# A graph network in fp32 on one core: the last block's products with the adjacency matrix on four row tiles

## The chip, the core and the metric

The kernel runs on one core of a Trainium2 chip. Its engines are named as the profile names them: PE (matrix products; PEld is its weight load), DVE (vector), ACT (scalar), POOL (GpSimd) and SP (here only a queue for DMAs). The metric is device time in microseconds (us).

## What is computed

Four layers in a row on 2708 nodes with 512 features. `adj` is a symmetric matrix of zeros and ones, 2708 x 2708, with about 0.6% ones. Cut to what matters:

```python
deg = jnp.maximum((adj != 0).sum(-1), 1.0)
# layer 0: degree-normalised sum over neighbours, times W, relu
x = layernorm(x + relu(((dinv * (adj + I) * dinv) @ x + x) @ W0 + b0))   # dinv: degree per row
# layer 1: the same with both sides scaled by deg ** -0.5
x = layernorm(x + ((dis * adj * dis) @ x) @ W1.T + b1)
# layer 2: two attention layers, softmax(scores) * adj, then @ Wh
x = layernorm(x + gat(gat(x)))
# layer 3: adj @ (H W) per head plus b, heads side by side
x = layernorm(x + adj @ (x @ W3) + b3)
```

Layers 0, 1 and 3 each hold one product of `adj` with the whole of `x`. The change is about these three products.

## The kernel before

**Tiling.** The 2708 nodes make 22 blocks of 128 rows (`NB`, `P`); block 21 has only 20 real rows (2708 - 21 x 128) and is padded with zeros. The output columns of a product with `adj` come in six chunks (`CH`): four of 512 columns, one of 384, one of 276. The 512 features are four groups (`DC`) of 128, numbered d. The 22 blocks are loaded in six groups (`GROUPS`): four of 4 blocks, two of 3. Block 21 is the last of group 5.

**The product.** `multiply` (L813) builds, for a chunk k, the four banks `acc[k][d]` (128 features x the chunk's columns), each summed over all 22 blocks. The weights are 128 columns of a block of x, the moving data are the block's rows of adj.T, cast to fp32r (tile `m`). To keep fp32 precision x is split by `halve` (L705) into two fp32r halves: `hi` (ACT, tiles named xh) and `lo = x*s - hi` (DVE, tiles named xl). Each block thus costs 4 x 2 = 8 products a chunk. In group 5 the products run d by d: for every d the blocks 19, 20, 21, each hi then lo. In chunk 0 the other groups run block by block.

**Loads.** `load` (L716) brings adj.T. In layer 0 it comes as fp32, one DMA of SP's queue per block, into a tile `at`; the pool of these tiles (`wides`) has 11 buffers, so a load waits until an older tile is free. In layers 1 and 3 it comes as bytes, one DMA per group, from `masks`, which layer 0 has written to memory.

**Preparing.** `prepare` (L749) casts `at` to `m` on ACT and, in chunk 0, calls `halve`. In layer 0 `examine` (L780) also makes bf16 copies (`some`, ACT), checks on DVE that all values are 0 or 1 (`odd`), makes the bytes for `masks` (POOL) and adds the blocks up into `part` (DVE), from which `degrees` (L836) gets the node degrees: `both` on DVE, a product with ones on PE (`deg`), then `dg` on DVE, then xt * dg on POOL, which `evict` (L869) adds to `acc` on DVE, giving `ht`. In layer 1 `prepare` also reduces the bytes to `feeds` (DVE), which says which 32-wide quarter of a block a node feeds.

**Order.** The order of issue on each engine is written out by hand: every instruction goes through `OrderedEngine` (L62), whose call on L70 keeps the order, which is why nearly all rows of the profile carry L70. `step` (L993) works through (layer, chunk, group): it loads two groups ahead and prepares one group ahead (`before_products`, L962), multiplies, and in between finishes the chunk before (`ends`, L1027: `project` gives the products mm with W, `combine` and `finish` the bias, the residual and the layer norm). In layer 3, chunks 0 to 2 begin while the attention layers end: groups 0 to 3 are multiplied early and saved to `begun`, groups 4 and 5 are added after.

**Tiles of the array.** `few` (L645) already uses a part of the array: where a block has at most 32 output rows, four products run on four column tiles (each a different quarter of the output partitions) and `total` adds the four parts. The lists of neighbours in `weigh` do the same with quarters of 32 rows.

Of the kernel before, what the change touches and what calls it, by code (L numbers as in the profile page):

```python
# [8 lines left out]
FP = mybir.dt.float32  # L9
# [10 lines left out]
P = 128  # L20
N = 2708
D = 512
NB = 22
NP = NB * P
DC = D // P
# [11 lines left out]
QUARTERS, QW = 4, P // 4  # L37
# [476 lines left out]
class Fast:  # L514
# [190 lines left out]
    def halve(self, ly, j):  # L705

        nc = self.nc
        hi = self.page(f"xh{ly.number}_{j}", FR)
        lo = self.page(f"xl{ly.number}_{j}", FR)
        s = self.k.dis[:, j : j + 1] if ly.number == 1 else 1.0  # L710
        x = ly.rows[j]
        nc.scalar.activation(hi, x, AF.Copy, scale=s)
        nc.vector.scalar_tensor_tensor(lo, x, s, hi.bitcast(FP), ALU.mult, ALU.subtract)
        ly.hi[j], ly.lo[j], ly.rows[j] = hi, lo, None

    def load(self, ly, k, g):  # L716

        c0, cw = CH[k]
        if (k, g) in ly.loaded:
            return  # L720
        ly.loaded.add((k, g))
        js = range(*GROUPS[g])
        if ly.number == 0:
            tiles = []
            for j in js:
                at = self.wide(f"at{ly.number}_{k}_{j}")
                self.nc.sync.dma_start(at[:, :cw], self.k.adj_t[bass.ts(j, P), c0 : c0 + cw])
                tiles.append(at)
        else:
            at = self.page(f"at{ly.number}_{k}_{g}", U8, (P, DC, BANK))  # L730
            self.nc.sync.dma_start(
                at[:, : len(js), :cw], self.k.masks[k][:, js[0] : js[-1] + 1, :]
            )
            tiles = [at[:, q, :] for q in range(len(js))]
            ly.done["bytes", k, g] = at
        ly.done["at", k, g] = tiles
        if k == 0 and ly.number == 0:
            for j in range(*GROUPS[g]):
                self.load_rows(ly, j)
        if k == 0 and ly.number == 3 and g < 4:  # L740
            for j in range(*GROUPS[g]):
                self.load_rows(ly, j)
        if ly.number == 0 and g == 2:
            xt = [self.page(f"xt{k}_{c}") for c in range(DC)]
            for c in range(DC):
                self.nc.gpsimd.dma_start(xt[c][:, :cw], self.k.x_t[:, c, c0 : c0 + cw])
            ly.done["xt", k] = xt

    def prepare(self, ly, k, g):  # L749


        nc, (c0, cw) = self.nc, CH[k]
        ats = ly.done.pop(("at", k, g), None)
        if ats is None:
            return
        ms = []
        for j, at in zip(range(*GROUPS[g]), ats):
            if k == 0:
                self.halve(ly, j)
            m = self.page(f"m{ly.number}_{k}_{j}", FR)  # L760
            nc.scalar.copy(m[:, :cw], at[:, :cw])
            ms.append(m)
        ly.done["m", k, g] = ms
        if ly.number == 0:
            self.examine(ly, k, g, ats)
        if ly.number == 1:
            at, (j0, j1) = ly.done.pop(("bytes", k, g)), GROUPS[g]
            feeds = self.k.feeds.rearrange("p i q j -> p j (i q)")
            i0, full = c0 // QW, cw // QW
            for q0, q1, n in ((0, full, QW), (full, -(-cw // QW), cw % QW)):  # L770
                if q0 < q1:
                    v = at[:, : j1 - j0, q0 * QW : q0 * QW + (q1 - q0) * n]
                    nc.vector.tensor_reduce(
                        feeds[:, j0:j1, i0 + q0 : i0 + q1],
                        v.rearrange("p j (q i) -> p j q i", i=n),
                        AX.X,
                        ALU.max,
                    )

    def examine(self, ly, k, g, ats):  # L780
        nc, cw = self.nc, CH[k][1]
        b0 = GROUPS[g][0]
        if g == 0:
            ly.part[k] = self.page(f"part{k}", BF, (P, 2, BANK))
        odd = self.page(f"odd{k}_{g}", BF)
        at_b = self.page(f"bytes{k}_{g}", U8, (P, DC, BANK))
        for q in range(0, len(ats), 2):
            some = self.page(f"some{k}_{g}_{q}", BF, (P, 2, BANK))
            m = min(2, len(ats) - q)
            for h in range(m):  # L790
                at = ats[q + h][:, :cw]
                n = k * NB + b0 + q + h
                nc.scalar.copy(some[:, h, :cw], at)
                nc.vector.scalar_tensor_tensor(
                    odd[:, :cw],
                    at,
                    1.0,
                    at,
                    ALU.is_equal,
                    ALU.not_equal,  # L800
                    accum_out=self.k.bad[:, n : n + 1],
                )
            nc.gpsimd.tensor_copy(at_b[:, q : q + m, :cw], some[:, :m, :cw])
            p = ly.part[k][:, :m, :cw]
            if b0 + q == 0:
                nc.vector.tensor_copy(p, some[:, :m, :cw])
            else:
                nc.vector.tensor_add(p, p, some[:, :m, :cw])
        nc.gpsimd.dma_start(
            self.k.masks[k][:, b0 : b0 + len(ats), :], at_b[:, : len(ats), :cw]  # L810
        )

    def multiply(self, ly, k, g, only=None):  # L813
        nc, cw = self.nc, CH[k][1]
        blocks = only or range(*GROUPS[g])
        two = ly.number == 3 and k < TWO
        starts, stops = ((0, 16), (15, NB - 1)) if two else ((0,), (NB - 1,))
        if blocks[0] in starts:

            half = 0 if two and blocks[0] == 0 else k  # L820
            ly.acc[k] = [self.bank(half, f"acc{ly.number}_{k}_{d}") for d in range(DC)]
        ms = ly.done["m", k, g]
        todo = [(d, j) for d in range(DC) for j in blocks]
        if k == 0 and g + 1 < len(GROUPS):
            todo.sort(key=lambda a: a[1])
        for d, j in todo:
            for x, first in ((ly.hi, True), (ly.lo, False)):
                nc.tensor.matmul(
                    ly.acc[k][d][:, :cw],
                    x[j][:, bass.ts(d, P)],  # L830
                    ms[j - GROUPS[g][0]][:, :cw],
                    start=(j in starts and first),
                    stop=(j in stops and not first),
                )
# [955 lines left out]
```

## Time and profile before

| what | value |
|---|---|
| median of 3 runs | 2413.58 us (2408.57 to 2414.01) |
| the profiled execution's own time | 2413.0 us |
| its span in the profile | 2411.3 us |
| granted PE clock, mean | 0.982 |
| layer 0, by the products' places in the timeline | 19 to 312 us |
| layer 1 | 312 to 617 us |
| attention, with early parts of layer 3 between | 618 to 2184 us |
| the rest of layer 3 | 2190 to 2396 us |
| products acc<-m,xh and acc<-m,xl | 1584 each, 588.7 and 574.5 us busy |

In the page, a group of instructions has its name as output<-inputs, its shape (for a product: rows*columns of the weights, then partitions x elements of the moving data), its count, its busy time, the mean of one, and the engine's idle time ahead of it with what ended it. The profile counts each fp32 product as two passes; an fp32r product is one. In a timeline the first two columns are the start and the length in us, and merged rows carry a count; "[0.31 <-ACT m]" is idle time ahead of the instruction and what ended it. "SPq" is SP's DMA queue.

### The profile page before, as it was taken

To read this page: it belongs to the slowest core of one execution; us is meant where nothing else is said; L and a number is where in the kernel's file an instruction comes from. 1 tells how busy PE (TensorE), PEld (TensorE's weight loads), DVE (VectorE), ACT (ScalarE), POOL (GpSimd) and SP (SyncE) were. 2 spreads that over 40 slices of the span, in tenths; PEclk is the share of its full clock that TensorE was granted. 3 is DMA by queue.
4 is the path that set the end of the run, shared out by engine and by line. 5 is a ranking of instruction groups with operands and counts; after the bars stand their busy time and mean duration, and the time that the engine had idled before them with its cause. 6 is when DMAs were issued, how large, how long until landed. Compare 5 with 4: busy or idle time off the path is not lost.

```text
span 2411.3 us, 26147 instructions
## 1 busy us (share of the span) xinstructions
PE 2305.6 (96%) x8518; PEld 1322.7 (55%) x8518; DVE 1475.1 (61%) x2842; ACT 653.8 (27%) x1300; POOL 770.3 (32%) x895
## 2 busy tenths in 40 slices
PE   8999999999999998999998999999999998899997
PEld 6677777777545443443554444444443454566685
DVE  7989984756535688757665511247868785623513
ACT  6444352321110122222222210123223233421121
POOL 6545541111000001634556450001643657451000
PEclk9999999999999999999999999999999998899999
DMA  9755552223454114868889895314967889872311
GB/s 349 253 182 165 175 174 77 77 75 110 150 189 181 47 53 126 297 224 284 269 292 353 269 387 207 130 40 154 325 215 270 307 273 345 247 251 93 115 54 41
DMA packets 311126, 471.74 MB, mean 196 GB/s; under 512 B 59874, under 2 KB 189418, under 8 KB 310980
## 3 DMA queue, kind: packets, MB, share of 16 engines
q1 hardware_dynamic: 249684, 236.61, 29.9%
q0 software_dynamic: 61296, 233.37, 28.0%
q8 instruction: 69, 1.13, 0.2%
q14 instruction: 77, 0.63, 0.1%
HBM read 316.01 MB, written 153.85 MB: 195 GB/s over the span
## 4 chain that ended last, share of the span: by engine, by line
PE 80%; DVE 10%; issue 3%; DMA 3%; ACT 1%; POOL 1%; SPq 1%; another core or an unknown queue 1%; DVEq 0%; ACTq 0%; POOLq 0%
PE acc L70 30%; PE sp L70 26%; PE mm L70 9%; PE wst L70 6%; PE z L70 6%; DVE s L70 2%; DVE sum L70 1%; SPq L70 1%; DMA pairs<-s 1%; DVE top L70 1%; DMA at<-in_adj_t 1%; DVE at_row L70 1%; DMA xt<-t 1%; DVE st L70 1%
## 5 line engine op out<-in xcount | busy, mean ns | idle before, releaser
L70 POOL DMA_INDIRECT g<-pairs,givers x510 | 516.3, 1012 | 955.5 <-issue 624.5
L70 PE MATMUL sp<-xs,wst_sb 128*128 128x512 f32 (+3 forms) x2112 | 805.2, 547 | 0.0
L70 PE MATMUL acc<-m,xh 128*128 128x512 f32 (+2 forms) x1584 | 588.7, 378 | 27.5 <-ACT begun L70 14.0
L70 PEld LDWEIGHTS sp<-xs,wst_sb 128*128 128x128 f32 (+1 forms) x2112 | 382.1, 187 | 403.4 <-issue 338.3
L70 PE MATMUL acc<-m,xl 128*128 128x512 f32 (+2 forms) x1584 | 574.5, 368 | 4.1 <-DVE xl L70 3.3
L70 PEld LDWEIGHTS acc<-m,xh 128*128 128x128 f32 x1584 | 301.7, 190 | 89.2 <-ACT begun L70 16.1
L70 PEld LDWEIGHTS acc<-m,xl 128*128 128x128 f32 x1584 | 302.2, 191 | 52.4 <-issue 6.2
L70 PE MATMUL acc<-g 128*32 128x512 f32 (+1 forms) x1020 | 265.2, 610 | 10.0 <-DMA g<-pairs,givers 7.9
L70 ACT COPY s<-sp 128x512 f32<-128x512 f32 (+2 forms) x252 | 132.8, 529 | 469.2 <-PE sp L70 311.2
L70 DVE TENSOR_TENSOR top<-top,s 128x512 f32<-128x512 f32 (+5 forms) x240 | 149.5, 623 | 161.2 <-ACT s L70 112.4
L70 PE MATMUL mm<-w,ht 128*128 128x512 f32 (+1 forms) x528 | 226.1, 600 | 7.7 <-DVE ht L70 7.7
L70 ACT ACTIVATE s<-s 128x512 f32<-128x512 f32 (+3 forms) x264 | 150.4, 580 | 294.4 <-DVE s L70 204.7
L70 ACT CAST m<-at 128x512 fp32r<-128x512 uint8 (+5 forms) x396 | 199.1, 567 | 68.0 <-DMA at<-mask 42.3
L70 DVE TENSOR_TENSOR sum<-sum,s 128x512 f32<-128x512 f32 (+4 forms) x252 | 156.8, 622 | 39.4 <-issue 20.9
L70 DVE TENSOR_TENSOR s<-s,a 128x512 f32<-128x512 f32 (+3 forms) x264 | 165.9, 628 | 9.1
L70 DVE TENSOR_TENSOR s<-s,shift 128x512 f32<-128x512 f32 (+3 forms) x264 | 162.8, 620 | 10.3 <-ACT shift L70 10.3
L70 PEld LDWEIGHTS mm<-w,ht 128*128 128x128 f32 (+1 forms) x528 | 96.9, 188 | 126.6 <-issue 112.3
L70 PEld LDWEIGHTS acc<-g 128*32 128x32 f32 (+1 forms) x1020 | 77.1, 136 | 147.4 <-issue 125.0
L70 PE MATMUL wst<-xt,mixed 128*128 128x512 f32 (+2 forms) x384 | 150.5, 545 | 1.7 <-issue 1.7
L70 PE MATMUL z<-w,xt 128*128 128x512 f32 (+1 forms) x352 | 150.2, 595 | 0.0
L70 DVE COPY z_sb<-z 128x512 f32<-128x512 f32 (+1 forms) x44 | 30.3, 690 | 175.8 <-PE z L70 130.8
L70 POOL DMA_DIRECT2D x<-o x44 | 25.9, 595 | 349.8 <-DVE o L70 346.1
(159 smaller groups left out, 1662.0 us busy)
## 6 DMA issues: line engine op xcount, KB each, us to landing
pairs<-s SPq DMA_DIRECT2D x378, 128.0 KB
pairs<-z_sb SPq DMA_DIRECT2D x84, 512.0 KB
at<-in_adj_t SPq DMA_DIRECT2D x88, 256.0 KB
xres<-x POOLq DMA_DIRECT2D x44, 256.0 KB
x<-o POOLq DMA_DIRECT2D x43, 256.0 KB
x<-x POOLq DMA_DIRECT2D x35, 256.0 KB
at<-mask SPq DMA_DIRECT2D x32, 256.0 KB
xt<-t SPq DMA_DIRECT2D x32, 256.0 KB
```

The source lines that it names most:

```text
L70: ins = call(*args, **kw)
```

## The change

The products of block 21 are done on four row tiles of the array. Its weights use only the first 32 partitions (20 of them real rows), so the four feature groups d are laid on the four quarters of the partitions:

- `fold` copies columns d x 128 to (d + 1) x 128 of block 21's first 32 rows to partitions d x 32 to (d + 1) x 32 of a new page (four ACT copies a layer); in layer 1 the scale `dis` is laid out likewise by four DVE copies. `halve` then works on 128 columns of this page for both halves, not on 512.
- In layer 0 the first 32 rows of block 21's adj.T are loaded four times, once on each quarter (four DMAs of 32 rows in place of one of 128). The bytes in `masks` then hold the four copies, and layers 1 and 3 load them as they did.
- `multiply` issues the eight products of block 21 ahead of the rest of group 5: four hi products, d = 0 to 3, each with 32 partitions of weights and of adj.T and with its own bank, then four lo products. Blocks 19 and 20 follow d by d. The group's last product is now that of block 20.
- `examine` adds only 32 partitions of block 21 to `part`, and `prepare` reduces block 21 to `feeds` by instructions of its own, so that the copies don't count.

```diff
@@ halve
+        if j == NB - 1:
+            x, s = self.fold(ly, x, s)
+            hi, lo = hi[:, :P], lo[:, :P]
         nc.scalar.activation(hi, x, AF.Copy, scale=s)
         nc.vector.scalar_tensor_tensor(lo, x, s, hi.bitcast(FP), ALU.mult, ALU.subtract)
         ly.hi[j], ly.lo[j], ly.rows[j] = hi, lo, None
+
+    def fold(self, ly, x, s):
+        nc = self.nc
+        f = self.page(f"fold{ly.number}")[:, :P]
+        for d in range(DC):
+            nc.scalar.copy(f[d * QW : (d + 1) * QW], x[:QW, bass.ts(d, P)])
+        if ly.number == 1:
+            t = self.small.tile([P, 1], FP, tag="dis_f", name="dis_f")
+            for d in range(DC):
+                nc.vector.tensor_copy(t[d * QW : (d + 1) * QW], s[:QW])
+            s = t
+        return f, s
@@ load
-                self.nc.sync.dma_start(at[:, :cw], self.k.adj_t[bass.ts(j, P), c0 : c0 + cw])
                 tiles.append(at)
+                if j < NB - 1:
+                    self.nc.sync.dma_start(
+                        at[:, :cw], self.k.adj_t[bass.ts(j, P), c0 : c0 + cw]
+                    )
+                    continue
+                few = self.k.adj_t[j * P : j * P + QW, c0 : c0 + cw]
+                for d in range(DC):
+                    self.nc.sync.dma_start(at[d * QW : (d + 1) * QW, :cw], few)
@@ prepare
+            sets = [(j0, j1, P)] if j1 < NB else [(j0, j1 - 1, P), (j1 - 1, j1, QW)]
             for q0, q1, n in ((0, full, QW), (full, -(-cw // QW), cw % QW)):
-                if q0 < q1:
-                    v = at[:, : j1 - j0, q0 * QW : q0 * QW + (q1 - q0) * n]
+                for a, b, rows in sets if q0 < q1 else ():
+                    v = at[:rows, a - j0 : b - j0, q0 * QW : q0 * QW + (q1 - q0) * n]
                     nc.vector.tensor_reduce(
-                        feeds[:, j0:j1, i0 + q0 : i0 + q1],
+                        feeds[:rows, a:b, i0 + q0 : i0 + q1],
@@ examine
-            p = ly.part[k][:, :m, :cw]
+            n = QW if b0 + q == NB - 1 else P
+            p, t = ly.part[k][:n, :m, :cw], some[:n, :m, :cw]
@@ multiply
-        starts, stops = ((0, 16), (15, NB - 1)) if two else ((0,), (NB - 1,))
+        starts, stops = ((0, 16), (15, NB - 2)) if two else ((0,), (NB - 2,))
         ms = ly.done["m", k, g]
+        if blocks[-1] == NB - 1:
+            blocks = blocks[:-1]
+            for x in (ly.hi, ly.lo):
+                for d in range(DC):
+                    few = slice(d * QW, (d + 1) * QW)
+                    nc.tensor.matmul(
+                        ly.acc[k][d][:, :cw],
+                        x[NB - 1][few],
+                        ms[-1][few, :cw],
+                        start=False,
+                        stop=False,
+                    )
```

More of the change, by code (lines that the diff above doesn't have):

```diff
@@ L803, in examine @@
             nc.gpsimd.tensor_copy(at_b[:, q : q + m, :cw], some[:, :m, :cw])
-            p = ly.part[k][:, :m, :cw]
+            n = QW if b0 + q == NB - 1 else P
+            p, t = ly.part[k][:n, :m, :cw], some[:n, :m, :cw]
             if b0 + q == 0:
-                nc.vector.tensor_copy(p, some[:, :m, :cw])
+                nc.vector.tensor_copy(p, t)
             else:
-                nc.vector.tensor_add(p, p, some[:, :m, :cw])
+                nc.vector.tensor_add(p, p, t)
         nc.gpsimd.dma_start(
```

## The prediction

> **What bounds the kernel now.** First the page's shares of busy time, to see which engine could be the bound:
> ```profile
> span 2411.3 us, 26147 instructions
> PE 2305.6 (96%) x8518; PEld 1322.7 (55%) x8518; DVE 1475.1 (61%) x2842; ACT 653.8 (27%) x1300; POOL 770.3 (32%) x895
> ```
> PE is busy in 96% of the span, so work taken off PE counts unless another engine ends that stage. Next the groups by shape give the size of what is edited; only the rows for the high halves are shown, those for the low halves have the same counts:
> ```profile
> L70 PE MATMUL acc<-m,xh 128*128 128x512 f32 x1056 | 430.1, 407 | 27.5 <-ACT begun L70 14.0 <-ACT m L70 8.6 <-DVE dg L70 4.9
> L70 PE MATMUL acc<-m,xh 128*128 128x384 f32 x264 | 89.9, 341 | 0.0
> L70 PE MATMUL acc<-m,xh 128*128 128x276 f32 x264 | 68.7, 296 | 0.0
> ```
> The mean of one (407 ns) holds latency that overlaps. The pitch is read from the chain that ended last, where whole runs of these products stand:
> ```profile
> 90.81 32.69 PE acc L70 x144
> ...
> 252.88 24.99 PE acc L70 x144
> ...
> 2369.89 18.48 PE acc L70 x144
> ```
> 32.69/144 = 0.227 us at 512 columns, 24.99/144 = 0.1735 at 384, 18.48/144 = 0.128 at 276. These runs are on the chain from end to end: there PE waits for nobody.
>
> **What is removed.** In each of 3 layers x 6 chunks, block 21 has 4 (d) x 2 (halves) = 8 products. At the pitches they take 8 x 0.227 = 1.82 us (12 chunks of 512), 1.39 (3 of 384), 1.03 (3 of 276): 29.0 us in all. They become two rounds of four products, each on 32 rows, each of the four into its own PSUM bank.
>
> **What a round costs.** No row of this trace has four row tiles. The nearest is the kernel's own set of four column tiles (`few`, 20 rows): same array, split the other way, fp32 in two passes. The timelines around one, of weight loads and of matmuls:
> ```profile
> 330.86 0.19 PEld L70 LDWEIGHTS mm<-w,ht 128*128 128x128 f32 x1 [0.24 <-issue]
> 331.81 0.14 PEld L70 LDWEIGHTS mm<-w,ht 128*20 128x20 f32 x8 [0.76 <-issue]
> 332.80 0.19 PEld L70 LDWEIGHTS acc<-m,xh 128*128 128x128 f32 x1 [0.85 <-issue]
> ```
> ```profile
> 331.29 1.58 PE L70 MATMUL mm<-w,ht 128*128 128x512 f32 x9
> 332.80 0.50 PE L70 MATMUL acc<-m,xh 128*128 128x512 f32 x1
> 333.13 0.40 PE L70 MATMUL acc<-m,xl 128*128 128x512 f32 x1
> ```
> The last full pass starts at 331.29 and at 0.43 us a pass (8 passes fill 3.43 us in the chain) is fed until 331.72. The second product after the set starts at 333.13, so the first had its normal slot from 332.90. Between lie 1.18 us for eight column-tiled passes. Two rounds of 0.43 are 0.86: four tiles do run side by side, and going into and out of the split costs 0.32 to 0.33. A load of 128 columns, which the row tiles need, adds what the first full product pays after the set (333.13 - 332.80 - 0.227 = 0.10). So I take 0.43 + 2 pitches: 0.88 us at 512 (gain 0.93), 0.78 at 384 (gain 0.61), 0.69 at 276 (gain 0.34). Sum: 12 x 0.93 + 3 x 0.61 + 3 x 0.34 = 14.0 us.
>
> Both bounds of this unknown: with no cost of the split it is 2 pitches, and 29.0 less a quarter is 21.8 us gained; with tiles that take turns and a load in front of each, 0.33 + 8 x 0.10 = 1.13 us is lost per chunk. I stay near the column-tiled row.
>
> A rule speaks against this. The Trainium skill ("TensorE: Matmul & The Clock Gate", section on LDWEIGHTS) has a weight load take its columns / 1.2 GHz, whatever the rows: a 32x128 load costs as much as 128x128, 107 ns. A full product hides it behind its own 0.227 us, but a round of four has four loads behind one 0.227 us. In line, eight loads are 0.86 us, and a chunk's set is 0.33 + 0.86 + one pitch: 1.41, 1.36 and 1.31 us, gains of 0.41, 0.03 and -0.28. Against it stands a row where four tiles get 32 columns each:
> ```profile
> 1014.57 0.16 PEld L70 LDWEIGHTS acc<-g 128*32 128x32 f32 x8 [0.76 <-issue]
> ```
> Eight loads are over in 0.16 us, latency included; in line the rule wants 8 x 27 = 0.21 us. So loads into different tiles overlap, and the second round's are taken ahead of the first round's products. I take overlapping loads for row tiles too, with doubt: column tiles are no row tiles.
>
> **Where the gain doesn't reach the end.** Layer 0, chunk 0, in the timelines of PE, ACT and DVE:
> ```profile
> 58.21 0.50 PE L70 MATMUL acc<-m,xh 128*128 128x512 f32 x1 [0.31 <-ACT m L70]
> 68.92 0.50 PE L70 MATMUL acc<-m,xh 128*128 128x512 f32 x1 [1.70 <-DVE dg L70]
> ```
> ```profile
> 57.56 0.60 ACT L70 CAST m<-at 128x512 fp32r<-128x512 f32 x1
> ```
> ```profile
> 68.18 0.69 DVE L70 TENSOR_SCALAR dg<-deg 128x512 f32<-128x512 f32 x1
> ```
> Block 21 is now first of its group and so waits for the last cast (57.56 + 0.60) with all 24 products behind it, where before four products of blocks 19 and 20 could go ahead. But dg reads the degree product that PE issued at 63.03 only at 68.18: DVE has no gap there, and 5 us of cover lie behind PE. Gain 0, and a loss of half a microsecond costs 0. Layer 0, chunk 5: PE's degree product is out at 312.16, dg runs at 316.27 behind four xl and a reduction, and PE sits idle until 316.75: gain 0 (0.34 lost). In the other layer-0 chunks DVE is busy 51.2 of 54 us (131 to 185), but it waited three times, 6.3 us in all, for PE's degree product between 75 and 240, so PE starts that chain and an earlier PE passes on. In layer 1 DVE is at some 60%. In layer 3 the stops before 2236.61 are a chain PE, `combine`, `ht`, which starts earlier as a whole. 14.0 - 0.93 - 0.34 = 12.7 us.
>
> **What is added elsewhere.** `fold`: four ACT copies of 32x128 a layer. ACT casts cost 0.61 us at 512 columns and 0.405 at 276, 0.87 ns a column, so 0.28 at 128: 1.1 us, less 0.34 that xh loses: +0.8 us of ACT. xl loses about 0.4 of DVE. Layer 1 also has four DVE copies of one column (128x4 took 0.15): 0.6 us, and xh waits for them; behind xh on ACT are m of block 21 and the next step's casts. Cover: in layer 1 xl of block 21 began at 357 to 358 and its products at about 361.4, 3 us; in layer 3, 2198.5 against 2201.4, 2.9 us. Without the cover it would be 1.4 us in one place and 0.8 in the other. Chunk 0 of layer 0 is told above. Loads: three more DMAs a chunk on SP, 18 in all, at 0.33 us of queue: 1 us a chunk, ahead of the next group's loads of adj.T. SP mostly waits for free tiles:
> ```profile
> SPq L70 <- DVE odd L70: 181.8, 92, 13.0
> ```
> and ACT waited for an adj.T load only once after 75 us, 0.5 us. Bytes are the same. I take 0; at worst 6 x 1 us. Seven more reductions for `feeds` in layer 1 (fixed part 0.12 us, from 2.29 us for 2048 elements and 0.21 for 80) are 0.8 us of an engine with 40% free: 0. The `part` sums shorten only in partitions: 0. One page more a layer shifts the reuse of pages; I know no row for that, from a slightly earlier to a slightly later load: 0.
>
> **The sum.** The profiled execution took 2413.0 us for its span of 2411.3 (1.7 around it); the median is 2413.6, 0.6 above, no more than runs differ. 2413.6 - 12.7 = 2400.9: forecast 2401.
>
> **Rivals.**
> - Loads in line, as the rule says. Eleven chunks of 512 gain 0.41, three of 384 gain 0.03, two of 276 lose 0.28 (the third is covered): 4.0 us, 2409.6. For it: [...]no trace here shows them; against it: the 0.16 us above. Chance 0.20.
> - Layer 0 gives nothing, DVE being next at 95%: 3.4 us (3 x 0.93 + 0.61) of the 12.7 go: 2404. For it the 51.2 of 54; against it the waits of DVE for PE. 0.12.
> - Slower: the row tiles take turns, since all four stream through the same 128 columns. Its place is each chunk's set; its price 0.33 + 8 x 0.10 us; 17 uncovered chunks x 1.13 = 19 us: 2433. It decides as soon as a product in the set costs over (1.82 - 0.43)/8 = 0.174 us, that is, when four tiles are less than 1.3 times as fast as one. Against it: four column tiles were about three times as fast. 0.11.
>
> **How the numbers follow.** The main case has 0.57. A measurement of this kernel can tell about 0.3% from no change, 7.2 us. Faster by more: the main case, most of the second rival, little of the first: 0.66. Within: most of the first rival, the rest of the second: 0.24. Slower: 0.10. The range runs from 2395 (a split that costs half of what I took) to 2411 (loads in line, plus a few late waits), which leaves out the case of turns and a little of either tail.
>
> **What would show it.** Groups acc<-m with 32 rows, 72 for each half; a chunk's run of 144 products at 512 columns shorter by 0.93 us; the eight tiled loads within some 0.3 us (loads in line would spread over 0.86); second-round products 0.23 us after the first round's; PE's idle time as before, with the wait for ACT m at 58 us longer. I would be wrong if the tiled loads stood 0.1 us apart, if products of one round started 0.2 us apart, or if PE's wait for DVE grew in layer 0 by what PE saved.

## The result, and the profile after

The changed kernel took 2403.4 us (median of 9 runs, 2396.2 to 2405.3), the kernel before 2414.0 (9 runs). The ratio is 0.9954, 95% interval 0.9942 to 0.9966. On 2414 us that is 11.1 us less, 8.2 to 14.0 (the medians differ by 10.6). The forecast was 12.7 us less.

The groups of products with `adj` in the profile after, by shape (count, then busy us and mean ns of one):
```profile
L70 PE MATMUL acc<-m,xh 128*128 128x512 f32 x1008 | 412.2, 409 | 26.4 <-ACT begun L70 14.7 <-ACT m L70 8.2 <-DVE dg L70 3.5
L70 PE MATMUL acc<-m,xh 32*128 32x512 f32 x48 | 6.1, 494 | 3.3 <-ACT m L70 3.3
L70 PE MATMUL acc<-m,xl 32*128 32x512 f32 x48 | 4.9, 391 | 0.0
```
48 of 1056 hi products at 512 columns are now 32 rows high, 12 in each of the two narrower widths. 4.9 us of busy time for 48 lo products is 0.10 us each, for something that takes 0.39 us from start to end: they overlap. The chain that ended last has the same whole runs of 144 products, now with a tiled set in each. First the run of this chunk before, then two runs after:
```profile
144.92 32.65 PE acc L70 x144
```
```profile
144.01 31.74 PE acc L70 x144
...
2352.97 18.10 PE acc L70 x144
```
That is 0.91 us less at 512 columns, and 0.38 less at 276, where such a run took 18.48 before. One set, in the timelines of PE and of its weight loads:
```profile
117.46 0.39 PE L70 MATMUL acc<-m,xh 128*128 128x512 f32 x1
117.69 0.39 PE L70 MATMUL acc<-m,xl 128*128 128x512 f32 x1
118.00 0.51 PE L70 MATMUL acc<-m,xh 32*128 32x512 f32 x4
118.34 0.41 PE L70 MATMUL acc<-m,xl 32*128 32x512 f32 x4
118.68 0.50 PE L70 MATMUL acc<-m,xh 128*128 128x512 f32 x1
119.02 0.40 PE L70 MATMUL acc<-m,xl 128*128 128x512 f32 x1
```
```profile
118.00 0.19 PEld L70 LDWEIGHTS acc<-m,xh 32*128 32x128 f32 x4 [0.35 <-issue]
118.11 0.19 PEld L70 LDWEIGHTS acc<-m,xl 32*128 32x128 f32 x4
118.67 0.19 PEld L70 LDWEIGHTS acc<-m,xh 128*128 128x128 f32 x1 [0.37 <-issue]
```
Four loads are over in 0.19 us, where one alone takes 0.18 to 0.19, and the second round's four start 0.11 us after the first's. From 117.69 to 119.02 are 1.33 us; less the slots of the two full products around the set (2 x 0.227) the set costs 0.88 us. By the starts in these rows it can be read as 0.08 to come out of the full array, 0.11 for the first loads, 0.23 for round 1, 0.23 for round 2, 0.11 to go back, and 0.11 for the next full load, which nothing hides.

By stages, from the places of the products in the two timelines:

| stretch | before | after | difference | forecast |
|---|---|---|---|---|
| first product with `adj` to chunk 5's degree product | 292.7 | 288.2 | -4.5 | -3.4 |
| to the first product of the attention layers (layer 1) | 305.9 | 301.6 | -4.3 | -4.7 |
| to the last gathered product (attention) | 1565.6 | 1562.6 | -3.0 | 0 |
| to the last product with W3 (rest of layer 3) | 211.9 | 205.0 | -6.9 | -4.7 |

The start was 1.4 us later after (20.8 against 19.4). The profiled execution of after, 2396.2 us, is the shortest of its nine runs, so this table overstates the gain. Part of what exceeds the forecast is not in the sets. The 32 passes of mm that begin chunk 1 of layer 0 took 15.1 us before and 13.4 after, from the first start to the last, and those of layer 3's second chunk 15.0 and 13.4. The granted PE clock over these passes was 0.89 before and 1.00 after. The same changed kernel, run again below, took 15.1 us at 0.89 in both places, so these 3.3 us belong to the executions and not to the change. Nothing was changed in the attention layers; their 3.0 us are not explained.

### The profile page after: what moved, and what is told of

It reads as the page before. It is cut to its first block, busy times and chain, and to the rows that moved or that the text cites. A ratio compares the mean times of both kernels' runs of the same rounds, so it can differ in the third digit from the quotient of the medians.

```text
span 2394.4 us, 26205 instructions
## 1 busy us (share of the span) xinstructions
PE 2292.1 (96%) x8518; PEld 1302.0 (54%) x8518; DVE 1474.3 (62%) x2853; ACT 657.3 (27%) x1312; POOL 772.7 (32%) x895
## 4 chain that ended last, share of the span: by engine, by line
PE 79%; DVE 9%; DMA 5%; issue 3%; ACT 1%; POOL 1%; SPq 1%; another core or an unknown queue 1%; DVEq 0%; POOLq 0%; ACTq 0%
PE acc L70 29%; PE sp L70 27%; PE mm L70 9%; PE wst L70 6%; PE z L70 6%; DVE s L70 2%; DMA at<-in_adj_t 2%; DMA pairs<-s 1%; DVE sum L70 1%; SPq L70 1%; DVE at_row L70 1%; DVE top L70 1%; DVE st L70 1%; DMA w<-in_w 1%
## 5 line engine op out<-in xcount | busy, mean ns | idle before, releaser
L70 PE MATMUL acc<-m,xh 128*128 128x512 f32 (+4 forms) x1584 | 573.3, 383 | 29.7 <-ACT begun L70 14.7
L70 PE MATMUL acc<-m,xl 128*128 128x512 f32 (+4 forms) x1584 | 555.8, 369 | 3.1 <-DVE xl L70 3.1
L70 PEld LDWEIGHTS acc<-m,xh 128*128 128x128 f32 (+1 forms) x1584 | 291.9, 190 | 99.0 <-issue 22.9
L70 PEld LDWEIGHTS acc<-m,xl 128*128 128x128 f32 (+1 forms) x1584 | 292.0, 191 | 49.7 <-issue 6.0
L70 ACT ACTIVATE s<-s 128x512 f32<-128x512 f32 (+3 forms) x264 | 150.3, 580 | 292.7 <-DVE s L70 203.7
L70 DVE TENSOR_TENSOR s<-s,shift 128x512 f32<-128x512 f32 (+3 forms) x264 | 162.7, 619 | 10.6 <-ACT shift L70 10.6
```

The costliest lines, as they stand in the source:

```text
L70: ins = call(*args, **kw)
```

## The experiments

There were ten runs, the last three of them of kernels that had run before, in three groups, each group on one chip with runs of the kernel before. That kernel took 2384.4, 2408.3 and 2386.5 us (medians) there, so the times expected on the base of 2414 have to be read as differences. All times below are differences to before in the same group, with the interval of the ratio.

**One row tile.** The kernel before (no `fold`, one load a block), with the eight products of block 21 first in their group, on 32 rows, all on the first quarter of the partitions. Cut from `multiply`:
```diff
+        if blocks[-1] == NB - 1:
+            blocks = blocks[:-1]
+            for x in (ly.hi, ly.lo):
+                for d in range(DC):
+                    nc.tensor.matmul(
+                        ly.acc[k][d][:, :cw],
+                        x[NB - 1][:QW, bass.ts(d, P)],
+                        ms[-1][:QW, :cw],
+                        ...
```


> Before, with block 21's eight products first in their group, on 32 rows, but all on the first quarter of the partitions, one row tile, without fold and with one load. My theory (a set costs 0.43 us for the split plus one pitch per round, and the gain comes from four tiles side by side): eight rounds in place of two, 0.43 us a chunk more than before, 16 chunks on the path: 2414 + 7 = 2421 us; if loads into one tile can't overlap with its product, 0.1 us a product more, 2433. Rival (fewer rows alone make a product cheaper): faster than 2414.

Measured: 1.0042 of before (1.0028 to 1.0056), 10.0 us more (6.7 to 13.4). The set in its timelines, products first, then loads:
```profile
116.44 0.39 PE L70 MATMUL acc<-m,xl 128*128 128x512 f32 x1
116.76 1.20 PE L70 MATMUL acc<-m,xh 32*128 32x512 f32 x4
117.80 1.07 PE L70 MATMUL acc<-m,xl 32*128 32x512 f32 x4
118.81 0.50 PE L70 MATMUL acc<-m,xh 128*128 128x512 f32 x1
119.14 0.40 PE L70 MATMUL acc<-m,xl 128*128 128x512 f32 x1
```
```profile
116.76 0.76 PEld L70 LDWEIGHTS acc<-m,xh 32*128 32x128 f32 x4 [0.35 <-issue]
117.57 0.87 PEld L70 LDWEIGHTS acc<-m,xl 32*128 32x128 f32 x4
```
The set costs 2.70 - 0.45 = 2.25 us = 0.43 + 8 x 0.227. So a product of 32 rows is not cheaper than one of 128, and the split costs the same 0.43 us with no tiles side by side. A load into the tile that is at work is still hidden (no 0.1 us a product). This is also the form in which the change would have been slower. The sets explain 16 x 0.43 = 6.9 us of it, at the low end of the interval.

**The order alone.** As above, with `x[NB - 1][:, bass.ts(d, P)]` and `ms[-1][:, :cw]`, on all 128 rows.

> Before, with only the order of the change: block 21's products first in their group, four hi then four lo, on all 128 rows. My theory: the same PE work, 2414 us. Rival (the order gives part of the gain, or costs at the waits for block 21's cast): 2410 or less, or 2417 and more.

Measured: 1.0005 (0.9997 to 1.0014), 1.2 us more (-0.7 to 3.3). Putting block 21 first neither gains nor costs anything that shows.

**Two splits a chunk.** The changed kernel, with the hi round first in the group and the lo round last (cut):
```diff
-            for x in (ly.hi, ly.lo):
-                ...
+            self.tiled(ly, k, ly.hi, ms, False)    # four products, d = 0 to 3
         ...
+        if last:
+            self.tiled(ly, k, ly.lo, ms, True)
```


> After, with the four hi products first in the group and the four lo products last, so that the array is split twice a chunk. My theory: a second split of 0.43 us in each of 16 chunks on the path, 2403 + 7 = 2410 us, and in the timeline each set at 0.43 us plus one pitch. Rival (a split costs nothing, the set is slow for another reason): 2403.

Measured: 0.9982 (0.9973 to 0.9991), 4.3 us less (2.1 to 6.4). Expected were 12.7 less the price of a second split in 16 chunks, 6.9: 5.8. PE around a round by itself (the profile joins the hi product behind it to its row):
```profile
117.33 0.39 PE L70 MATMUL acc<-m,xl 128*128 128x512 f32 x1
117.64 0.94 PE L70 MATMUL acc<-m,xh 32*128 32x512 f32 x5
118.42 0.39 PE L70 MATMUL acc<-m,xl 128*128 128x512 f32 x1
```
1.09 - 0.45 = 0.64 us: 0.41 for the split and 0.23 for the round. The split is paid once per place, not once per round.

**Halves stacked, no tiles.** lo lies under hi in one page, and one product of 128 rows adds both. Against the changed kernel, cut to what matters (`fold` is gone, and block 21 is back at its old place in the group):
```diff
         nc.scalar.activation(hi, x, AF.Copy, scale=s)
+        if j == NB - 1:
+            lo, x, hi = hi[QW : 2 * QW], x[:QW], hi[:QW]
             ...
@@ load
+                tail = self.k.adj_t[bass.ts(j, P), c0 : c0 + cw]
+                self.nc.sync.dma_start(at[:QW, :cw], tail[:QW])
+                self.nc.sync.dma_start(at[QW : 2 * QW, :cw], tail[:QW])
+                self.nc.sync.dma_start(at[2 * QW :, :cw], tail[2 * QW :])
@@ multiply
+            halves = ((ly.hi, True), (ly.lo, False)) if j < NB - 1 else ((ly.hi, False),)
```


> No tiles: block 21's lo half lies on partitions 32 to 63 under its hi half, its adj.T rows are loaded on both, and one product of 128 rows per d sums both halves: four products a chunk at the full pitch, no split. My theory (rounds times pitch, plus 0.43 only where the array is split): gains 0.91, 0.69 and 0.51 us at 512, 384 and 276 columns, 13.1 us in all: 2401, level with after within the measurement. Rival (the gain hangs on the tiles, or on work taken off ACT and DVE): 2410 or more.

Measured: 0.9970 (0.9958 to 0.9981), 7.2 us less (4.5 to 10.0), some 6 us short of the expectation. The shortfall is not in the sets. The groups by shape show that the lo products of block 21 are gone and the hi ones are of full height:
```profile
L70 PE MATMUL acc<-m,xh 128*128 128x512 f32 x1056 | 422.9, 407 | 19.0 <-ACT begun L70 9.5 <-ACT m L70 4.8 <-DVE dg L70 4.4
...
L70 PE MATMUL acc<-m,xl 128*128 128x512 f32 x1008 | 399.3, 396 | 3.6 <-DVE xl L70 3.6
```
Layer 1 took 301.2 us in its trace (301.6 in after's), but the second attention layer (from its first product mix to the last gathered product) 860.0, against 856.1 to 856.7 in the three kernels beside it. It was run again below.

**Block 21 left out.** The sums then lack 20 nodes. `todo = [(d, j) for d in range(DC) for j in blocks if j < NB - 1]` in before.

> Before, with block 21's products with adj left out in all three layers (the sums lack 20 nodes; the other work stays). It asks how much of saved PE time reaches the end. My theory (all but layer 0's chunks 0 and 5): 11 x 1.82 + 3 x 1.39 + 2 x 1.03 = 26.2 us of 29.0: 2388. Rival (DVE is next in layer 0 and the attention layers absorb some): less than 20 us, over 2394.

Measured: 0.9894 (0.9877 to 0.9911), 25.5 us less (21.4 to 29.6) of 29.0 saved on PE. Most of what PE saves in these places reaches the end.

**Left out in layer 0 only.**
```diff
+        end = NB - 2 if ly.number == 0 else NB - 1
         ...
-        todo = [(d, j) for d in range(DC) for j in blocks]
+        todo = [(d, j) for d in range(DC) for j in blocks if j <= end]
```


> Before, with block 21's products left out in layer 0 only. My theory (chunks 1 to 4 pass on what PE saves, 0 and 5 do not): 3 x 1.82 + 1.39 = 6.9 us: 2407. Rival (DVE bounds layer 0): 2412 or more; other rival (all chunks pass on): 2414 - 9.7 = 2404.

Measured: 0.9981 (0.9972 to 0.9991), 4.6 us less (2.2 to 6.7), below the 6.9 expected, which lies just beyond the interval: the theory was too generous here, and the rival that DVE bounds layer 0 has a part. From degree product to degree product, chunk by chunk:

| chunks of layer 0 | before | after | left out in layer 0 | PE work saved there |
|---|---|---|---|---|
| 1 to 2 (123.34 to 177.41 before) | 54.07 | 53.16 | 52.67 | 0.94 / 1.82 |
| 2 to 3 | 54.07 | 53.14 | 53.00 | 0.94 / 1.82 |
| 3 to 4 (384 columns) | 46.22 | 45.63 | 44.89 | 0.63 / 1.39 |

After passes on nearly all that it saves. Leaving more out gains 1.40 and 1.07 us where 1.82 were saved, and 1.33 of 1.39 in the narrower chunk; the kernel with block 21 left out everywhere gives 1.39, 1.04 and 1.31. The waits of DVE for PE's degree product between 75 and 240 us say why, before and after:
```profile
DVE dg L70 <- PE deg L70: 6.3, 3, 3.2
```
```profile
DVE dg L70 <- PE deg L70: 1.8, 3, 1.1
```
In the kernel with layer 0's products left out the row is gone, and DVE is busy 159.9 of these 165 us. DVE waited 6.3 us for PE before, 1.8 after, then not at all: it has become the bound. Of the fall to 1.8, 1.7 us are the faster mm passes of chunk 1 told above; in the later run of the changed kernel DVE waited 3.6 us, 2.7 less than before, about 0.9 for each of three chunks.

**The tiled set last in its group.** The changed kernel, with both rounds behind blocks 19 and 20 and `stop` on the lo round.

> After, with the tiled set last in its group, behind blocks 19 and 20. My theory: the set costs the same anywhere, and PE's wait of 3.3 us for block 21's cast in layer 0, chunk 0 shrinks to about 1.5 us but lies beside DVE: 2403, as after. Rival (that wait costs time at the end): 2401 or less.

Measured: 0.9942 (0.9927 to 0.9958), 14.0 us less (10.1 to 17.6). That interval overlaps with that of the changed kernel, so both were run side by side.

**The changed kernel, tiles last and stacked, on one chip.**

> The changed kernel as it is, on one chip with the next two. My theory: 0.995 of before, as measured, some 12 us.

> After with the tiled set last in its group, beside after. The product behind the set is then mostly one in bf16 (degree, rank, list), whose weight load is shorter: 0.1 us less in 11 chunks, about 1 us, plus what layer 0's chunk 0 gains. My theory: 1 to 2 us below after. Rival (the larger gain of the first run was chance): level with after; both can't be told apart surely within the measurement.

> The stacked halves beside after. If sets alone decide, level with after, 12 us below before. Rival (something outside the sets, in the attention layers, takes 4 us back whenever pages and loads are laid out this way): again 4 us or more above after, and the attention layers again longer in its trace than in that of after.

Measured: after 0.9956 (0.9943 to 0.9969), tiles last 0.9955 (0.9939 to 0.9972), stacked 0.9954 (0.9938 to 0.9970): 10.5, 10.7 and 11.0 us less. The three can't be told apart. A set behind which the degree product stands is cheaper, in the timeline of tiles last:
```profile
120.81 0.39 PE L70 MATMUL acc<-m,xl 128*128 128x512 f32 x1
121.13 0.51 PE L70 MATMUL acc<-m,xh 32*128 32x512 f32 x4
121.47 0.41 PE L70 MATMUL acc<-m,xl 32*128 32x512 f32 x4
121.80 0.39 PE L70 MATMUL deg<-both,ones_b 128*128 128x512 bf16 x1
122.03 0.24 PE L70 MATMUL cnt<-ones_b,both 128*128 128x1 bf16 x4
```
The weight load of the degree product's bf16 data took 0.10 us in the profile, against 0.19 for fp32r, and the next product starts a usual 0.23 us behind it. So the set costs 0.99 - 0.23 = 0.76 us where after's has 0.88, but some 1 us in all is less than a measurement shows. Stacked is level with the tiles in time here, though its second attention layer was long in this trace too (860.0 against 854.3 and 854.2 in the other two). Both stacked traces are of executions above their kernel's median, by 2.8 and 4.9 us. Why that layer was longer, and why the first group fell 6 us short, was not settled; the median of the second group shows no price of stacking.

## Why the prediction was right, and where it was off

- **The cost of a set.** Put at 0.43 us plus two pitches: 0.88, 0.78 and 0.69 us. The timelines after have 0.87, 0.76 and 0.65 (medians by width). The column-tiled set was the right row to go by, and the 0.10 added for a 128-column load was right: 0.11. Less two pitches the split costs 0.42, 0.41 and 0.39 us at the three widths; why it falls a little was not asked.
- **Loads side by side.** The rule of the Trainium skill ("TensorE: Matmul & The Clock Gate", section on LDWEIGHTS) holds for one load: a 32-row load takes 0.18 us in the profile and a 128-row load 0.19, and each costs 0.11 us where nothing hides it. That loads stand in line was a reading of it for the rival, and the runs show otherwise: what was read from the column tiles, that loads into different tiles overlap, holds for row tiles too. Loads in line would have made a set of 1.41 us.
- **Taking turns.** The slower rival is refuted by the starts: those of one round lie within 0.02 us, and the second round's 0.34 us after the first's. One row tile shows what it would have been like, at +10 us; the load in front of each product that it also assumed is hidden even there.
- **Where the gain stops.** Chunk 0 of layer 0 gained nothing, as told, but the loss on PE was mis-sized: put at half a microsecond, it was 1.9 us, counted from the first product to the degree product. PE waited 3.3 us for block 21's cast, which `fold` precedes on ACT, and behind that wait seven products followed each other 0.43 us apart in place of 0.227. The granted clock was 0.70 from 60.2 to 63.7 us:
```profile
60.27 0.50 PE L70 MATMUL acc<-m,xh 32*128 32x512 f32 x4 [3.27 <-ACT m L70]
...
62.30 0.63 PE L70 MATMUL acc<-m,xh 128*128 128x512 f32 x1
62.73 0.63 PE L70 MATMUL acc<-m,xl 128*128 128x512 f32 x1
```
The cover of 5 us held, with 3.6 us left between PE's degree product (66.33) and dg:
```profile
69.90 0.69 DVE L70 TENSOR_SCALAR dg<-deg 128x512 f32<-128x512 f32 x1
```
In chunk 5 PE still waits for dg, 3.48 us (3.23 before), so nothing is gained there. Chunks 1 to 4 pass on nearly all their gain, against the second rival; that DVE there was near its limit was seen, but how near only the left-out kernel showed. PE's waits for DVE between 75 and 312 us were 4.9 us before and 5.4 after, so they did not grow by what PE saved.
- **Costs elsewhere.** `fold` took four ACT copies of 0.30 us (1.22 together, put at 1.1), xh fell from 0.63 to 0.31, the four DVE copies took 0.6, though ACT waited 1.6 us for them in layer 1, the cover taking it. The products of block 21 in layers 1 and 3 (358.9 and 2192.9 us) started without a wait. ACT waited for no adj.T load after 75 us.
- **The size.** 12.7 was forecast, 11.1 (8.2 to 14.0) and 10.5 (7.4 to 13.6) measured. The difference lies within the intervals, and no term of the sum is shown to be too large. The mechanism is confirmed by the sets themselves; that the total came so near is in part luck, since single executions differ by 3.3 us in the mm passes alone.

## What to carry to other kernels

A short block in a sum costs PE a full product per output group: 0.227 us with 32 rows as with 128. Here four of them on four row tiles, each with its own PSUM bank, ran in the time of one, plus 0.43 us for leaving and re-entering the full array, so put all rounds of a split in one place. Where the same rows are multiplied twice (hi and lo halves), stacking the halves in one full-height product saves half of them without any split, here for the same gain. Before asking for more of the same, look at who waits for PE: here DVE's wait of 6.3 us was gone once block 21's products were left out of layer 0, and of the 9.7 us of PE work that this saved 4.6 reached the end.

## What the runs showed that was not expected

- The kernel before took 2384 to 2414 us in groups of runs on different chips. In the traces layers 0 and 1 take about the same time; the attention layers took 1565.6 us in before's trace and 1539.2 in that of the kernel with only the order changed, which does the same work on another chip. The traces of one group, on one chip, lie within 6 us of each other there (1558 to 1561 in the second group). A difference of 11 us can only be read beside runs on the same chip.
- A wait of PE can cost more than its own length. Behind the wait of 2.3 us before chunk 1 of layer 0, passes of mm stood 0.85 us apart for a while in before's trace and at their usual 0.43 in after's; in the later run of the changed kernel they were slow again. What decides it was not asked.
- Behind a split a bf16 product costs 0.1 us less than an fp32r one: it shows no exposed load.
- Coming out of the full array and going back cost about 0.1 us each; the rest of the 0.43 us is two weight loads of 0.11 us that nothing hides.
